# A decoder layer with Mamba, experts, cross-attention and FP8 FFN on one core: half of values × Wo moved into the scan, the sums of the experts moved into the attention pipeline

## The chip, the core and the metric

The kernel runs on one core of one Trainium2 chip, as one program. The metric is the time of one execution on the device in microseconds (us). A core has a matrix engine (TensorE, PE in the profile, with its weight loads as PEld), a vector engine (VectorE, DVE), a scalar engine (ScalarE, ACT), a general one (GpSimd, POOL) and SyncE (SP), which issues transfers. Each runs its own list of instructions in order, and they wait for each other on semaphores. Transfers (DMAs) are issued from an engine's list and then run beside all of them. SBUF is the on-chip memory, PSUM the memory that TensorE writes to.

## The reference

The input is `x` [4, 256, 256], four sequences of 256 tokens with 256 features, and a context of 4 × 64 positions with 128 features. Cut to what matters:

```python
# 1 Mamba mixer, then experts
xz = rmsnorm(x) @ in_proj.T                  # 256 -> 1024
xc = silu(causal_conv(x_half)); dt, B, C = split(xc @ x_proj.T)   # then rmsnorm of each
dt = softplus(dt @ dt_proj.T + dt_b)
h_t = h_{t-1} * exp(dt_t * A) + dt_t * x_t * B_t                  # DI = 512, N = 16
y = (sum_n h_t C_t + xc * D_param) * silu(z)
r = y @ out_proj.T + x; flat = rmsnorm(r)
moe = sum over the top 2 of 8 experts e:  p_e * ((silu(flat @ w1[e].T) * (flat @ w3[e].T)) @ w2[e].T)
x = layernorm(x + moe)
# 2 cross-attention, 16 heads of 128
q, k = rmsnorm(x @ Wq), rmsnorm(ctx @ Wk);  v = ctx @ Wv
x = layernorm(x + softmax(q k^T / sqrt(128)) v @ Wo)
# 3 gated FFN of 704, operands rounded to FP8 by row scales
x = layernorm(x + ffn(x))
```

## The kernel before

The 1024 tokens are 8 tiles of 128; `x_sb` holds all of them in SBUF. The stages follow each other, and the trace shows their bounds:

1. Prologue (0 to 60 us): norms, in_proj, convolution of the first half.
2. Scan (60 to 318 us): 64 steps `i`, the list `SL`; a step is one half of the tokens (`h`, 512 tokens), two of four chunks of channels (`c0`) and one state `n`. `M` = 32 is the first step of the second half. A step has `da` on ScalarE (L587), `dbx` on POOL (L595), the scan `hs` on VectorE (L654), its product with C, `hc`, on VectorE (L662) or, in 14 steps, POOL (L679), and the sum over states `py` on TensorE (L644). The row of B for a step, `bB`, comes by a DMA on SP three steps ahead (L577). Beside it runs `fill`, a chain of generators: work of the other stages cut into pieces by `yield`, of which each step takes one. All pieces share a pool of one PSUM bank, `ps1`, so a piece's matmuls can begin when the copy out of the piece before is done. In it are the second half's convolution and dt, then (from step M + 2) out_proj of the first half, its routing (`after_scan`), and in steps M + 18 to M + 21 the first two chunks of out_proj of the second half (`out_part`, matmuls p_op L426).
3. Rest of routing, keys and tables (318 to 402 us). K is folded with Wq here; the result, m_d, lies in HBM (a quarter, one sequence, is `mb`, 1 MB).
4. Expert slots (402 to 613 us): 23 slots of 128 token places, each with gate and up matmuls (p_gu L1121), transposes (p_hTa L1139, p_hTb L1144) and the down matmul (p_hTb L1151), and a write of the result `y` to `ys_d` in HBM (L1160).
5. Combine and values (613 to 650 us, L1207 to L1252). Each token's two expert rows are gathered from `ys_d` by 16 indirect DMAs on POOL (`yg`, L1214, two per tile). VectorE adds them with their gates (L1227), then a layernorm (L1233, L64 to L66, L1240). Beside it `prep_v` folds V with Wo for the attention: per group of `GQ` = 4 heads, `p_vT` = ctx · Wv (L814), a copy `vT` (L819), `p_vw` = v · Wo (L829), a copy to `vw_sb` (L835). Its weights (`cT_v`, four `wv_t`, four `wo_t`), Wq (`wq_sb`, L1193) and two `mb` (L1195) are loaded on SP when the last slot begins; the FFN's weights (L1218 to L1222) follow on SP.
6. Attention and FFN (650 to 855 us, L1258 to L1407): a software pipeline over tiles, in whose step `i` stand `stage_scores(i)`, `stage_attend(i - 1)`, `stage_up(i - 2)` and `stage_down(i - 3)`. Scores has the transposes p_x1T (L1274) and their copy x1T (L1275), p_q (L1280) with squares and their sums (L1285, L1286), p_sc (L1295) times the norm, and v minus its maximum on POOL (L1306). Attend multiplies with `vw_sb` (p_av L1327).

In the scan, the slots and the combine stage PE, DVE, ACT and POOL run in the order in which the code is written (`manual_schedule`). SP's order, and that of everything in stage 6, is set by a scheduler. Pools with `side="right"` lie at the other end of SBUF and are closed and opened as a stack.

These lines order stage 5: all gathers first, nine pieces of values, then per tile the sum, the norm of the tile before and two more pieces, and the rest before stage 6.

```python
pv.send(psV)
for _ in range(9):
    next(pv)
for t in range(NT):
    combine(t)
    if t:
        normed(t - 1)
    next(pv, None)
    next(pv, None)
normed(NT - 1)
run(pv)
```

Of the kernel before, what the change touches and what calls it, by code (L numbers as in the profile page):

```python
# [10 lines left out]
F32 = mybir.dt.float32  # L11
# [38 lines left out]
def decoder_kernel(  # L50
# [128 lines left out]

    flat_d = dram.tile([T, D], F32, name="flat_d")  # L180
# [4 lines left out]
    zs = mb.tile([P, NC, T], F32, name="zs")  # L185
    xc = mb.tile([P, NC, T], F32, name="xc")
    dt = mb.tile([P, NC, T], F32, name="dt")
    dtx = mb.tile([P, NC, T], F32, name="dtx")
# [60 lines left out]
    def conv_part(h, xpad, ps, early):  # L249
        cs = slice(h * HALF, (h + 1) * HALF)  # L250
        cw, cb = col("conv_w"), col("conv_b")
        acc = a1.tile([P, 2, HB, L], F32, tag="conv", name="conv") if early else None
        for c in (2, 3, 0, 1):
# [7 lines left out]
            else:  # L261
# [9 lines left out]
                xc[:, c, cs], v, AF.Silu if early else AF.Identity, bias=cb[:, c : c + 1]  # L271
            )
        if not early:
            yield
            nc.scalar.activation(xc[:, :, cs], xc[:, :, cs], AF.Silu)
            yield

    def z_part(h, hsT, ps):
        for c in range(NC):
# [6 lines left out]
            nc.scalar.copy(zs[:, c, h * HALF : (h + 1) * HALF], pt)  # L286

    def dt_part(h, hsT, ps, early):
# [7 lines left out]
        for i2 in range(HT // 2):  # L296
            pt = ps.tile([P, HALF], F32, tag="ps", name="p_xp")
            for i in range(2):
                t = h * HT + 2 * i2 + i
                for n, c in enumerate((2, 3, 0, 1)):  # L300
                    nc.tensor.matmul(
                        pt[:, i * W : (i + 1) * W], xc[:, c, t * P : (t + 1) * P], xpT[:, c, :],
# [54 lines left out]
        w = dtx[:, :, cs]  # L357
        b = col("dt_b")
        pairs = [slice(0, 2), slice(2, NC)]
        if early:  # L360
# [5 lines left out]
            with tc.manual_schedule(engines={ET.DVE, ET.Activation}):  # L366
                for c, pt in enumerate(pts):
                    nc.scalar.activation(u[:, c, :], pt, AF.Abs, bias=b[:, c : c + 1])
                    nc.vector.tensor_scalar(dt[:, c, cs], pt, b[:, c : c + 1], 0.0, add, ALU.max)
                for c in pairs:  # L370
# [3 lines left out]
                    nc.vector.tensor_tensor(dt[:, c, cs], dt[:, c, cs], u[:, c, :], sub)  # L374
# [5 lines left out]
                nc.vector.tensor_tensor(dt[:, c, cs], dt[:, c, cs], w[:, c, :], add)  # L380
                nc.vector.tensor_tensor(dtx[:, c, cs], dt[:, c, cs], xc[:, c, cs], mult)

            return
        for c in range(NC):
# [4 lines left out]
            nc.scalar.activation(dt[:, c, cs], pt, AF.Relu, bias=b[:, c : c + 1])  # L389
# [12 lines left out]
        for c in range(2):  # L402
            nc.gpsimd.tensor_tensor(dt[:, c, cs], dt[:, c, cs], u[:, c, :], sub)
        yield
        next(zp, None)
        for c in range(2, NC):
            nc.gpsimd.tensor_tensor(dt[:, c, cs], dt[:, c, cs], u[:, c, :], sub)
# [3 lines left out]
    def last_of_dt(h, chunks):  # L411
        cs = slice(h * HALF, (h + 1) * HALF)
        for c in chunks:
            nc.gpsimd.tensor_tensor(dt[:, c, cs], dt[:, c, cs], dtx[:, c, cs], add)
            nc.gpsimd.tensor_tensor(dtx[:, c, cs], dt[:, c, cs], xc[:, c, cs], mult)
            yield

    def out_part(h, ps, ob, chunks):
# [3 lines left out]
        for i in range(HT):  # L422
            t = h * HT + i
            pt = ps.tile([P, HALF], F32, tag="ps", name="p_op")
            for c in chunks:
                nc.tensor.matmul(  # L426
                    pt[:, 0:D], zs[:, c, t * P : (t + 1) * P], opT[:, c, :],
# [154 lines left out]
    def decay(i):  # L582
        h, c0, n = SL[i]
        cs = slice(h * HALF, (h + 1) * HALF)
# [893 lines left out]
```

## Time and profile before

| what | us |
|---|---|
| median of 3 runs | 852.98 (850.94 to 855.36) |
| profiled execution | 856.38 |
| its span in the trace | 854.7 |
| prologue, to | 60 |
| scan, to | 318 |
| routing, keys, tables, to | 402 |
| expert slots, to | 613 |
| combine and values, to | 650 |
| attention and FFN, to | 854.7 |

A profile is one execution. "Busy" is the time in which an engine executes; what it waits for is inferred from semaphores. Instructions are named by their output tile and by the line of the kernel. A matmul of 32-bit numbers shows as two records, so counts of records are twice those of the code there. TensorE's clock is throttled in some stages; the granted clock is given as a share. Further numbers from the trace: `hs` takes 2.28 us and there are 64, `hc` 1.22 on VectorE and 2.35 on POOL, `dbx` 2.35, `da` 2 × 0.69. In the combine stage VectorE's pieces per tile are two sums of 0.48, 0.43, 0.18, 0.15, 0.16 and 0.40, and ScalarE has a square root of 0.20 and one table load of 1.28. The first tile's p_q starts at 650.09, the second's at 663.12, the third's at 679.59; later steps of the pipeline take some 22 us each, with VectorE busy 19.

### The profile page before, as it was taken

The page shows a single profiled execution, that of the slowest core. Times are in us where ns is not written, and L with a number is a line of the kernel's source. Part 1 is how long each engine was busy: PE and PEld are TensorE (multiplying, and loading weights), DVE is VectorE, ACT ScalarE, POOL GpSimd, SP SyncE. Part 2 cuts the span into 40 slices and gives each one's busy share as a digit, 9 for nine tenths or more (in the row PEclk, how much of TensorE's full clock was granted, in tenths as well). Part 3 has the DMA queues.
Part 4 walks back from the last instruction along what each step waited for, and adds up shares of the span by engine and source line. Part 5 has one row for each costly group of instructions (what it writes and reads, how often), then busy time and mean ns, then how long its engine had stood idle before and what let it go on. Part 6 is the DMA issues. An engine that isn't in the chain of part 4 may idle for free.

```text
span 854.7 us, 8109 instructions
## 1 busy us (share of the span) xinstructions
PE 685.7 (80%) x2449; PEld 383.5 (45%) x2449; DVE 569.1 (67%) x959; ACT 341.4 (40%) x564; POOL 385.9 (45%) x278
## 2 busy tenths in 40 slices
PE   3968868778656776747999999999986998999963
PEld 1533433324322323635555656556642554555541
DVE  4468799997899993663335454555144578888885
ACT  3386654755533323322221112112233555555533
POOL 7039878899766860022012332222060334444451
PEclk9999998999877997767999999999997999999985
DMA  4023322256521308943022544232690101000000
GB/s 153 1 74 86 99 65 69 83 156 205 168 87 44 104 25 298 397 142 104 25 72 17 67 55 66 39 54 56 204 393 16 49 1 49 7 6 7 8 6 19
DMA packets 54954, 76.43 MB, mean 89 GB/s; under 512 B 15872, under 2 KB 35072, under 8 KB 54144
## 3 DMA queue, kind: packets, MB, share of 16 engines
q1 hardware_dynamic: 48048, 64.11, 23.8%
q0 software_dynamic: 2320, 6.56, 5.2%
q10 hardware_dynamic: 4544, 5.24, 1.8%
q8 instruction: 21, 0.34, 0.2%
q14 instruction: 21, 0.17, 0.1%
HBM read 64.22 MB, written 11.67 MB: 89 GB/s over the span
## 4 chain that ended last, share of the span: by engine, by line
PE 45%; DVE 26%; POOL 12%; issue 7%; ACT 6%; DMA 3%; ACTq 0%; POOLq 0%; DVEq 0%
PE p_gu L1121 12%; PE p_hTb L1151 8%; DVE hs L654 6%; PE py L644 5%; POOL dbx L595 4%; PE p_q L1280 3%; PE p_m L774 2%; DVE hc L662 2%; PE p_cv L264 2%; POOL v L1306 1%; PE p_gu L1361 1%; DMA wk_t<-in_wk_dram 1%; POOL yg L1214 1%; PE p_sc L1295 1%; DVE ssq L1286 1%
## 5 line engine op out<-in xcount | busy, mean ns | idle before, releaser
L595 POOL TENSOR_TENSOR dbx<-dtx,bB 128x1024 f32<-128x1024 f32 x64 | 149.4, 2354 | 23.7 <-DVE hs L654 12.5
L654 DVE TENSOR_TENSOR_SCAN hs<-da,dbx 128x1024 f32<-128x1024 f32 x64 | 145.5, 2281 | 17.0 <-POOL dbx L595 8.6
L644 PE MATMUL py<-hc,ident 128*128 128x512 f32 x256 | 134.1, 656 | 3.6 <-DVE yd L615 2.0
L1121 PE MATMUL p_gu<-w,xT 128*128 x276 | 119.2, 569 | 2.0 <-ACT xT L1111 2.0
L587 ACT ACTIVATE da<-dt,a_neg 128x510 f32<-128x510 f32 x128 | 87.7, 688 | 77.6 <-DVE hs L654 75.4
L644 PEld LDWEIGHTS py<-hc,ident 128*128 128x128 f32 x256 | 52.9, 208 | 113.8 <-issue 101.0
L606 PE MATMUL pC<-bc,sel 96*128 96x512 bf16 x50 | 20.5, 409 | 66.1 <-DVE hc L662 65.3
L1121 PEld LDWEIGHTS p_gu<-w,xT 128*128 128x128 f32 x276 | 49.9, 194 | 44.0 <-issue 34.6
L1151 PE MATMUL p_hTb<-w2r,hT 128*128 (+1 forms) x276 | 67.9, 387 | 0.7 <-ACT hT L1140 0.7
L662 DVE TENSOR_TENSOR hc<-hs,pC 128x1024 f32<-128x1024 f32 x50 | 61.1, 1221 | 4.8
L1280 PE MATMUL p_q<-wq_sb,x1T 128*128 128x512 f32 x128 | 58.8, 613 | 4.8 <-ACT x1T L1275 4.8
L1151 PEld LDWEIGHTS p_hTb<-w2r,hT 128*128 128x128 f32 (+1 forms) x276 | 50.4, 189 | 19.1 <-issue 7.6
L1132 DVE TENSOR_TENSOR h<-sg,p_gu 128x704 f32<-128x704 f32 x23 | 20.4, 888 | 42.1 <-ACT sg L1130 42.1
L1140 ACT COPY hT<-p_hTa 128x512 f32<-128x512 f32 x23 | 13.5, 586 | 83.1 <-PE p_hTa L1139 76.0
L917 POOL DMA_INDIRECT xs<-flat_d,tok_i x23 | 22.7, 986 | 43.0 <-PE p_xT L1109 28.4
L1280 PEld LDWEIGHTS p_q<-wq_sb,x1T 128*128 128x128 f32 x128 | 24.4, 195 | 34.6 <-issue 26.9
L85 POOL TENSOR_TENSOR wgu<-wgu,w_m 128x512 f32<-128x512 f32 (+1 forms) x6 | 7.6, 1267 | 71.3 <-DVE w_m L84 71.3
L1147 DVE COPY hT<-p_hTb 128x128 f32<-128x128 f32 (+1 forms) x46 | 11.0, 281 | 41.4 <-PE p_hTb L1144 41.4
L679 POOL TENSOR_TENSOR hc<-hs,cB 128x1024 f32<-128x1024 f32 x14 | 32.9, 2350 | 8.9 <-issue 5.3
L1306 POOL TENSOR_TENSOR v<-v,st 128x1024 f32<-128x1024 f32 x8 | 15.2, 1902 | 48.0 <-DVE st L1305 48.0
L1285 ACT ACTIVATE q<-p_q 128x512 f32<-128x512 f32 x32 | 18.9, 594 | 34.1 <-PE p_q L1280 26.5
L1214 POOL DMA_INDIRECT yg<-ys_d,yrow_i x16 | 15.4, 965 | 37.2 <-PE p_vT L814 32.6
(331 smaller groups left out, 1278.0 us busy)
## 6 DMA issues: line engine op xcount, KB each, us to landing
bB<-b_d SPq DMA_DIRECT2D x64, 256.0 KB, 3.2
w<-in_w1T_dram SPq DMA_DIRECT2D x2, 2816.0 KB, 21.5
w<-in_w3T_dram SPq DMA_DIRECT2D x2, 2816.0 KB, 25.3
w2r<-in_w2T_dram SPq DMA_DIRECT2D x8, 640.0 KB, 5.6
m_d<-mst SPq DMA_DIRECT2D x8, 512.0 KB, 2.9
mb<-m_d SPq DMA_DIRECT2D x4, 1024.0 KB, 8.2
cB<-b_d SPq DMA_DIRECT2D x14, 256.0 KB, 3.3
ys_d<-y SPq DMA_DIRECT2D x21, 128.0 KB, 1.7
```

The lines of the kernel that those rows point to most:

```text
L587: nc.scalar.activation(das[i % 2][:, j, :, 1:], dt[:, c, cs].rearrange("p (b l) -> p b l", l=L)[:, :, 1:], AF.Exp, scale=a_neg[:, c * N + ...
L595: nc.gpsimd.tensor_tensor(dbxs[i], dtx[:, c0 : c0 + 2, h * HALF : (h + 1) * HALF], bBs.pop(i).unsqueeze(1).to_broadcast(two), mult)
L644: nc.tensor.matmul(ys[i][j], ident, hc[:, j, :], start=(n == 0), stop=(n == N - 1))
L654: nc.vector.tensor_tensor_scan(hs, das[i % 2].rearrange("p c b l -> p (c b l)"), dbxs.pop(i).rearrange("p c t -> p (c t)"), 0.0, mult, add,)
L662: nc.vector.tensor_tensor(hcs[i], hv, pcs.pop(i).unsqueeze(1).to_broadcast(two), mult)
L679: nc.gpsimd.tensor_tensor(hcs[i], hv, cBs.pop(i).unsqueeze(1).to_broadcast(two), mult)
L917: nc.gpsimd.indirect_dma_start(out=xs[s], out_offset=None, in_=flat_d, in_offset=bass.IndirectOffsetOnAxis(ap=tok_i[:, s : s + 1], axis=0),)
L1121: nc.tensor.matmul(pt[:, c, 0:w], x[:, k, :], w13[k][:, bass.DynSlice(ex[s], 1), o : o + w].rearrange("p e i -> p (e i)"), start=(k == 0), ...
L1151: nc.tensor.matmul(po, hT[:w, i, :], w2r[:w, i, bass.DynSlice(ex[s], 1), :].rearrange("p e d -> p (e d)"), start=(i == 0), stop=(i == NI - 1),
L1214: nc.gpsimd.indirect_dma_start(out=y, out_offset=None, in_=ys_d, in_offset=bass.IndirectOffsetOnAxis(ap=yrow_i[:, j, t : t + 1], axis=0),)
L1280: nc.tensor.matmul(pq, x1T[:, k, :], wq_sb[:, k, q * HALF : (q + 1) * HALF], start=(k == 0), stop=(k == KD - 1),)
L1306: nc.gpsimd.tensor_tensor(v, v, st[:, 0].unsqueeze(2).to_broadcast(full), sub)
```

## The change

Values × Wo is split in two. The heads 0 to 7 (groups 0 and 1) are done in the scan's `fill` chain, one piece a step (some steps take two), after the first half's routing. What they give is copied by ScalarE to a small buffer and written to HBM (`vw_d`, 8 writes of 256 KB on SP, `park`). The heads 8 to 15 stay where they were, behind the last slot. Their pieces use the PSUM pool of the attention pipeline. The two chunks of out_proj of the second half come after the values in the chain, in the last four steps of the scan. The tiles xc, dt, dtx of the first half move to a pool of their own on the right side (`h0p`), which is closed at step M + 2, four steps later than the pool that was closed there before; so w2's loads begin three steps later.

After the slots POOL issues the gathers of tiles 0 and 1, then the load of `vw_d` into `vw_sb` (2 MB), gathers of tiles 2 and 3, the FFN's weights (3 MB in six DMAs, before on SP), gathers of 4 and 5, the second `mb` (1 MB, before on SP), gathers of 6 and 7. The sums and norms of tiles 0 and 1 come before the pipeline; that of tile `i` + 2 stands in the pipeline's step `i`, ahead of `stage_scores(i)`.

```diff
@@ pools @@
+    vw_d = dram.tile([B, P, H // 4, D], F32, name="vw_d")
...
-    xc = mb.tile([P, NC, T], F32, name="xc")
-    dt = mb.tile([P, NC, T], F32, name="dt")
-    dtx = mb.tile([P, NC, T], F32, name="dtx")
+    h0p = h0ctx.enter_context(tc.tile_pool(name="h0p", bufs=1, side="right"))
+    hp = (h0p, mb)
+    xc = [hp[h].tile([P, NC, HALF], F32, name=f"xc{h}") for h in range(2)]
+    dt = [hp[h].tile([P, NC, HALF], F32, name=f"dt{h}") for h in range(2)]
+    dtx = [hp[h].tile([P, NC, HALF], F32, name=f"dtx{h}") for h in range(2)]
...
@@ ahead of the scan loop @@
+    def prep_v(vp, groups, put):
+        cT = vp.tile([P, B * S], F32, name="cT_v")
+        nc.sync.dma_start(cT, ctxT)
+        ws = {}
+        for q in groups:
+            wt = vp.tile([P, HALF], F32, tag="wv_t", name="wv_t", bufs=len(groups))
+            nc.sync.dma_start(wt, wv[:, q * HALF : (q + 1) * HALF])
+            w2 = vp.tile([P, GQ, D], F32, tag="wo_t", name="wo_t", bufs=len(groups))
+            nc.sync.dma_start(w2, wo[q * HALF : (q + 1) * HALF, :].rearrange("(h p) d -> p h d", p=P))
+            ws[q] = wt, w2
+        ps = yield
+        yield
+        for q in groups:
+            wt, w2 = ws.pop(q)
+            vT = vp.tile([P, GQ, B * S], F32, tag="vT", name="vT")
+            for j in range(0, GQ, 2):
+                pt = ps.tile([P, HALF], F32, tag="ps", name="p_vT")
+                for o in range(2):
+                    nc.tensor.matmul(
+                        pt[:, o * B * S : (o + 1) * B * S], wt[:, (j + o) * HD : (j + o + 1) * HD], cT,
+                        start=True, stop=True,
+                    )
+                yield
+                nc.scalar.copy(vT[:, j : j + 2, :].rearrange("p h s -> p (h s)"), pt)
+            for j in range(GQ // 2):
+                for b2 in range(B // 2):
+                    pt = ps.tile([P, HALF], F32, tag="ps", name="p_vw")
+                    for b in range(2):
+                        for o in range(2):
+                            bb = 2 * b2 + b
+                            nc.tensor.matmul(
+                                pt[o * S : (o + 1) * S, b * D : (b + 1) * D],
+                                vT[:, 2 * j + o, bb * S : (bb + 1) * S], w2[:, 2 * j + o, :],
+                                start=True, stop=True,
+                            )
+                    yield
+                    put(2 * b2, q * (GQ // 2) + j, pt.rearrange("p (b d) -> p b d", d=D))
+
+    def park(b, pr, v):
+        st = vp.tile([P, 2, D], F32, tag="vw_st", name="vw_st", bufs=2)
+        nc.scalar.copy(st, v)
+        nc.sync.dma_start(vw_d[b : b + 2, :, pr, :].rearrange("b p d -> p b d"), st)
...
@@ in the scan loop @@
+            if i == M + 2:
                 pctx.close()
+                h0ctx.close()
...
+                early_values = prep_v(vp, range(2), park)
+                next(early_values)
...
             if i == M + 2:
-                fill = itertools.chain(fill, out_part(0, ps1, ob, range(NC)), after_scan(0, ps1, ob, False))
-            if i == M + N + 2:
-                fill = itertools.chain(fill, out_part(1, ps1, ob, range(2)))
+                early_values.send(ps1)
+                fill = itertools.chain(
+                    fill, out_part(0, ps1, ob, range(NC)), after_scan(0, ps1, ob, False),
+                    early_values, out_part(1, ps1, ob, range(2)),
+                )
             next(fill, None)
-            if i > M and i % 3 == 0 and (i - M) // 3 < E:
-                load_w2((i - M) // 3)
+            if i in (M + 10, M + 15):
+                next(fill, None)
+            if i > M + 2 and i % 3 == 0 and (i - M - 3) // 3 < E:
+                load_w2((i - M - 3) // 3)
...
@@ in the last slot @@
-                pv = prep_v(vp, vw_sb)
-                next(pv)
+                late_values = prep_v(
+                    vp, range(2, H // GQ), lambda b, pr, v: nc.scalar.copy(vw_sb[:, b : b + 2, pr, :], v)
+                )
+                next(late_values)
                 nc.sync.dma_start(wq_sb, wq.rearrange("(k p) c -> p k c", p=P))
-                for b in range(2):
-                    nc.sync.dma_start(mbs[b], m_d[b].rearrange("p k h s -> p k (h s)"))
+                nc.sync.dma_start(mbs[0], m_d[0].rearrange("p k h s -> p k (h s)"))
...
@@ in place of the combine stage @@
+    def load_ffn():
         for j in range(2):
+            nc.gpsimd.dma_start(wgu[j], wgu_d[j])
+            nc.gpsimd.dma_start(wdn[j], wdn_d[j])
+        nc.gpsimd.dma_start(sgu_row, sgu_d.unsqueeze(0).to_broadcast([P, 2, I]))
+        nc.gpsimd.dma_start(sdn_row, sdn_d.unsqueeze(0).to_broadcast([P, D]))
...
+        def combine(t):
+            if t < NT:
+                for j in range(2):
+                    nc.vector.scalar_tensor_tensor(
+                        x_sb[:, t, :], ygs.pop((t, j)), g2[:, j, t : t + 1], x_sb[:, t, :], mult, add
+                    )
+                layernorm(x_sb, t, wk2)
+
+        with tc.manual_schedule(engines={ET.PE, ET.DVE, ET.Activation, ET.Pool}):
+            for t in range(NT):
+                for j in range(2):
+                    y = ygs[t, j] = wk2.tile([P, D], F32, tag="yg", name="yg", bufs=2 * NT)
+                    nc.gpsimd.indirect_dma_start(
+                        out=y, out_offset=None, in_=ys_d,
+                        in_offset=bass.IndirectOffsetOnAxis(ap=yrow_i[:, j, t : t + 1], axis=0),
+                    )
+
+                if t == 1:
+                    nc.gpsimd.dma_start(
+                        vw_sb[:, :, 0 : H // 4, :].rearrange("p b h d -> p b (h d)"),
+                        vw_d.rearrange("b p h d -> p b (h d)"),
+                    )
+                if t == 3:
+                    load_ffn()
+                if t == 5:
+                    nc.gpsimd.dma_start(mbs[1], m_d[1].rearrange("p k h s -> p k (h s)"))
+            late_values.send(ps)
+            for _ in range(8):
+                next(late_values)
+            combine(0)
+            for _ in range(3):
+                next(late_values)
+            combine(1)
+            run(late_values)
...
@@ in the pipeline loop @@
+                combine(i + 2)
                 vs[i] = stage_scores(i)
```

## The prediction

> **What bounds the kernel now.** I read the page's busy row first, then busy time by stage, then, for the stage that the change takes apart, its timeline, its chain of waits and its list of waits.
>
> ```profile
> PE 685.7 (80%) x2449; PEld 383.5 (45%) x2449; DVE 569.1 (67%) x959; ACT 341.4 (40%) x564; POOL 385.9 (45%) x278
> ```
>
> TensorE at 80% is an average. By stage (start:end, length, busy us of PE, PEld, DVE, ACT, POOL, granted clock, DMA share, GB/s):
>
> ```profile
> 253.00:305.00 52.00, 33.72 (x76) 15.35 (x76) 48.15 (x47) 17.94 (x26) 38.67 (x18) 0.82 0.24 72
> 402.00:613.00 211.00, 207.62 (x790) 123.27 (x790) 94.13 (x249) 41.80 (x81) 48.47 (x45) 0.99 0.33 55
> 613.00:650.00 37.00, 24.89 (x163) 15.53 (x162) 17.54 (x57) 15.72 (x34) 15.44 (x16) 0.87 0.80 305
> 650.00:680.00 30.00, 28.36 (x77) 14.38 (x78) 14.47 (x26) 13.16 (x21) 5.71 (x3) 0.94 0.10 36
> 733.00:821.50 88.50, 78.06 (x363) 47.88 (x362) 75.94 (x162) 49.41 (x79) 39.57 (x29) 1.00 0.02 7
> ```
>
> Rows: end of the scan (VectorE full, TensorE a third idle); expert slots (TensorE 98%); combine and values (no engine full, DMA 80%); start of the attention pipeline (TensorE full, VectorE half idle); its steady part (VectorE 86%, TensorE 88%). The 37 us of the third row are the ones to win.
>
> ```profile
> 613.61 0.33 ACTq L1160 DMA_DIRECT2D ys_d<-y  x1
> 622.23 0.95 POOL L1214 DMA_INDIRECT yg<-ys_d,yrow_i  x1 [32.64 <-PE p_vT L814]
> 629.03 0.48 DVE L1227 SCALAR_TENSOR_TENSOR x_sb<-yg,g,x_sb 128x256 f32<-128x256 f32 x1 [15.45 <-DMA yg<-ys_d,yrow_i]
> 648.90 0.69 PE L1274 MATMUL p_x1T<-ident,x_sb 128*128 128x128 f32 x2 [7.51 <-ACT vw_sb L835]
> ```
>
> Columns: start, duration, engine, line, tile, idle time before and its releaser. The last slot writes its result at 613.61; the first gather, G below, starts at 622.23. The releaser named there only came last: in the program the gather waits for that write, so the write took 8.6 us. Tile 0 of attention starts at 648.90. From the chain of waits:
>
> ```profile
> 634.73 0.94 POOL yg L1214
> 635.67 0.30 issue
> 635.98 5.87 DMA yg<-ys_d,yrow_i
> 641.94 0.50 DVE x_sb L1227
> ...
> 648.28 0.58 ACT vw_sb L835
> 648.90 0.70 PE p_x1T L1274 x2
> ```
>
> Sixteen gathers at 0.95 + 0.30 us stand in a row, then a landing of 5.87, then VectorE's sums of the last tiles, then the last values copy, and only then tile 0. Tile 0's two gathers land by 630; it waits for tile 7's. The waits of the stage (total, times, longest) say the same:
>
> ```profile
> DVE x_sb L1227 <- DMA yg<-ys_d,yrow_i: 16.7, 4, 15.4
> PE p_x1T L1274 <- ACT vw_sb L835: 7.5, 1, 7.5
> ```
>
> **What the Trainium skill says.** "DMA: Bandwidth & Descriptors", section "Anatomy of one DMA — SWDGE (gpsimd) path": a DMA issued by GpSimd costs about 2.0 us fixed plus bytes over 436 GB/s, and making its descriptors is a small, varying part. The trace has 2.8 us as the shortest landing of a gather, 5.9 as the median; and POOL's time for one hardly depends on its rows:
>
> ```profile
> 508.63 0.91 POOL L996 DMA_INDIRECT wgu<-in_w_gu_dram,idx_dn  x1 [0.30 <-issue]
> 509.84 0.95 POOL L917 DMA_INDIRECT xs<-flat_d,tok_i  x1 [0.30 <-PE p_wT L1024]
> ```
>
> The first moves 64 rows, the second 128. "Perfetto Trace Analysis", section "DMA Instruction — SWDGE (GPSIMD)", takes such an instruction's end as the end of its descriptors, not the arrival of data: agrees (0.94 against 5.87 above). "SBUF — State Buffer", box "DVE blocks DMA": GpSimd can't write descriptors while VectorE runs an operation in its two-port mode; no run yet shows plain loads from POOL beside a busy VectorE, so this is a risk, not a price. "ScalarE: Activation LUTs", section "What ACT_TABLE_LOAD costs": about 1.28 us; the trace has 1.28.
>
> **The change part by part.** Everything is against the profiled execution: 856.38 us, span 854.7; the median of the runs is 852.98, 3.4 less, and I carry the difference over unchanged.
>
> *G, the first gather.* In the changed order three matmuls of the late p_vT stand ahead of the last slot's second transposes, and wait for cT_v and wv_t. The first wv_t is issued at 606.47 and lands in 5.8 to 7.4 us (its tile's row: 5.8/6.6/7.4), so about 612.8, where TensorE would be there at 609: the slot's end moves by +3.3 + 0.7 (two more p_vT, at 0.24 a record and two records a matmul, with their weights). Queued behind are the slot's p_hTa/p_hTb, y and its write. Against that, the write then meets less: before, weights for attention and FFN were queued on SP up to 624.7; now SP carries 4.63 MB (cT, two wv, two wo, wq, mb0), which at 390 GB/s (the best two slices of the page have 393 and 397) are 11.9 us from 606, so nearly gone at 617.6. Landing 3 in place of 8.6: −5.6. Sum −1.6; I take −1.5 (−3.5 if wv_t lands early, +1 if the write gains only 3).
>
> *Tile 0's start.* Before G + 27.86 (first p_q at 650.09). After: the gathers of tiles 0 and 1 are the first four. Gather 2 issued at G + 2.5; landing 4 (2.8 to 5.9), two sums of 0.48, norm 1.32 with a table load of 1.28 that is exposed, square root 0.20, transposes 0.70, copy 0.38, small gaps about 0.8: G + 12.5 (11.6 to 14.5). The late values, half of 7.7 + 16.8 = 12.2 us (busy time of p_vT and p_vw in this stage), lie beside G's wait and landings on TensorE, which has nothing else. −15.4.
>
> *What is late next: POOL's queue.* It now holds 16 gathers, vw_sb (2 MB), six FFN loads (3 MB), mb1 (1 MB) = 24 DMAs, and behind them tile 0's v minus its maximum. With a DMA at b = 1.25 us it ends at G + 30; the maximum of tile 0 is done 14.9 after its first p_q (664.96 before), G + 27.4. Sums of tiles 4 to 7 stand on VectorE inside tile 1's squares (start about G + 25.5); the last gather lands G + 32 to 35. From first p_q to tile 2's took 29.5 us before (650.09 to 679.59), with VectorE busy 3.37 of 12.5 in the first step. I take +0.5 (−0.5 to +2.5). Each further us in b costs 8: from then on the queue is the bound. All of it in bytes, 8 MB with the gathers at 390 GB/s, takes 20.5 us, so bytes are not the limit.
>
> *Sums of tiles 2 to 7 in the pipeline.* The two sums of tiles 2 and 3 (0.96 each) fall in the first step's idle VectorE. The norms (0.43 + 0.18 + 0.15 + 0.16 + 0.40 = 1.32) of tiles 4 to 7 fall in steps 2 to 5, of 17 to 28 us, where VectorE is on the path (15.34 of 21.8 in 679–701, 27.85 of 32 in 701–733): 5.3, a quarter of it hidden: +4 (+1 to +5.3). The number of table loads stays.
>
> *Scan.* Added to steps 47 to 59: 4 p_vT pieces (3.84 us, 0.96 each), 8 p_vw pieces (8.4, 1.05 each), 12 ScalarE copies of 0.58, 8 writes of 256 KB and 1.6 MB of loads on SP. TensorE gets 12.2 in the first row's 18 idle us, less 4.1 of out_part's second half that leaves it; ScalarE gets 7.0 of 34 idle; DMA is at 24%. VectorE, the bound, gets nothing: hidden, though with 80% TensorE is no longer far from the step. Not hidden: out_part's second half, four matmuls of 1.03 each, now comes in the last four steps, where TensorE's tail (12 py, 314.11 to 319.42) sets the end: the last one's 1.03, and 1 for single waits: +2 (−2 since VectorE's wait of 2.57 us for p_op at 278.80 may go; +5 if all four p_op and a wait count). On SP each write stands ahead of later loads of bB, 0.33 us an issue; these are sent three steps ahead, and a landing takes 3.2.
>
> *Slots* keep their instructions but for the last one (counted under G).
>
> Sum: −1.5 − 15.4 + 0.5 + 4 + 2 = −10.4. Profiled execution 846.0; median 842.6, so **843**.
>
> **The rivals.**
> A, as summed: 843; own range 838 (G −3.5, norms +1) to 848 (queue +2.5, scan +5).
>
> B, POOL's queue becomes the bound. For it: plain loads of 2 MB have no row from POOL, and descriptors may starve; and the loads' order would put the gathers of tiles 2 to 7 behind 2, 5 and 6 MB. Against: 64 and 128 rows cost the same. With b = 2.3: 8 × 1.05 = +8.4, 851; b = 2.6 gives back everything (+10.8).
> C, slower: the pieces of values lie on the scan's step, because a single PSUM bank makes each wait for the copy before it and pulls py, and with it hc's buffers and VectorE, along. Price: 12.2 + 12 × 0.58 + 4 × 1.03 = 23.3, and 8 issues of 0.33 ahead of bB = 2.6; 25.9 in place of 2 gives 867. It decides once the scan grows by more than 16.7 (857.3). For it: a p_vw piece is as long as a p_op piece (1.03), and VectorE waited for one of those. Against: that wait came from the copy on VectorE, which here is on ScalarE; TensorE is a third idle, and the same bank carries a piece a step before the change with VectorE at 92%.
> D, more than forecast: norms hidden altogether (−4) or no delay of the last slot (−3.5): about 839 and below.
> That the change does not do what it says, all gathers still waited for by tile 0 through a shared buffer, is excluded: sixteen buffers, and sums in tile order.
>
> **How the numbers follow.** A 0.59, B 0.18, C 0.09, D 0.14. 0.5% is 4.3 us, about what can be told from no change: faster means below 848.7. A and D lie there, and 0.04 of B: 0.77. The rest of B: same, 0.14. C: slower, 0.09. The range 835 to 853 takes in A, most of D and the better part of B, leaving out C, b of 2.6 and above and a sum of D's two gains.
>
> **What would show it.** Tile 0's first p_q 12 to 13 us after the first gather and about 17 earlier than 650; VectorE's long wait for gathers split into one before tile 0 and little in tile 1; POOL's DMAs 1.25 apart, plain ones too; the scan's hs still back to back and its last py within 2 us of 319.4; pipeline steps 2 to 5 longer by about 1 each. Wrong would be: plain POOL loads of 2 us or more with v waiting behind them, hs with gaps in steps 47 to 63, or a first gather later than 624.

## The result, and the profile after

| | before | after |
|---|---|---|
| median | 853.48 (4 runs, 850.94 to 855.36) | 843.48 (4 runs, 842.79 to 845.77) |
| ratio, 95% interval | | 0.9868 [0.9843, 0.9894] |
| span of the profiled execution | 854.7 | 843.6 |

10.0 us less by the medians, 11.1 by the two traces, against a forecast of 10.4 (843). The granted clock is not the same in every execution of one kernel: the scan's last `yd` ended between 320.7 and 326.1 us in the traces of this study with the scan of before or of after (from 110 to 150 us the clock was 0.91 in before's trace and 0.84 in that of `late_only`, whose scan is the same). So single traces are compared below stage by stage, each stage from its own start. The page's busy row, and the same stages of the changed kernel's trace as were shown of before (start:end, length, busy us of PE, PEld, DVE, ACT, POOL, granted clock, DMA share, GB/s):

```profile
PE 683.3 (81%) x2449; PEld 379.0 (45%) x2449; DVE 563.2 (67%) x959; ACT 341.2 (40%) x564; POOL 391.2 (46%) x286
```

```profile
253.00:305.00 52.00, 44.13 (x143) 19.73 (x143) 46.15 (x37) 23.06 (x37) 44.10 (x21) 0.87 0.38 117
398.00:610.00 212.00, 209.00 (x798) 124.31 (x797) 94.41 (x250) 41.88 (x80) 47.69 (x44) 0.99 0.35 58
610.00:631.50 21.50, 12.04 (x76) 6.70 (x74) 4.69 (x15) 7.95 (x15) 10.20 (x12) 0.78 0.68 253
631.50:665.50 34.00, 29.87 (x76) 15.21 (x76) 21.46 (x43) 13.03 (x21) 15.89 (x16) 0.89 0.53 199
```

The combine stage is 21.5 us in place of 37; TensorE has 10.4 us more work in the scan's end, where it had been a third idle; the first two steps of the pipeline last some 34 us in place of 30, with VectorE busy for 21.5 in place of 14.5. Its timeline around the start of tile 0 (start, duration, engine, line, tile, idle time before and its releaser):

```profile
605.12 0.67 PE L657 MATMUL p_vT<-cT_v,wv_t 128*128 128x256 f32 x2 [0.41 <-DMA wv_t<-in_wv_dram]
...
610.43 0.33 ACTq L1167 DMA_DIRECT2D ys_d<-y  x1
...
619.17 0.95 POOL L1240 DMA_INDIRECT yg<-ys_d,yrow_i  x1 [32.56 <-DMA mb<-m_d]
...
622.21 0.48 DVE L1231 SCALAR_TENSOR_TENSOR x_sb<-yg,g,x_sb 128x256 f32<-128x256 f32 x1 [12.05 <-DMA yg<-ys_d,yrow_i]
...
623.88 0.83 POOL L1246 DMA_DIRECT2D vw_sb<-vw_d  x1
...
624.89 1.28 ACT L66 ACT_TABLE_LOAD   x1 [9.22 <-DVE ln_rs L65]
...
626.29 0.57 ACT L662 COPY vT<-p_vT 128x512 f32<-128x512 f32 x1
...
626.91 3.68 PE L669 MATMUL p_vw<-wo_t,vT 128*64 128x256 f32 x16 [9.18 <-ACT vT L662]
...
630.52 0.69 PE L1274 MATMUL p_x1T<-ident,x_sb 128*128 128x128 f32 x2
```

Read from above: the late p_vT waited 0.41 us; the write still took 8.7 us until the first gather. The releaser named there, mb's load, only landed last, 0.3 after the write; in `write_first` below the gather starts while that load is still under way. Tile 0 no longer waits for tile 7's gathers, but its last wait is again for the values, since a copy of vT stands on ScalarE behind the square root of tile 0's norm and TensorE idles 9.2 us for it. A plain load of 2 MB costs POOL 0.83 us, not more than a gather.

The stages of the profiled executions of all kernels in this study, from the timeline. "Keys" is from the end of the last `yd` to the first slot's p_xT; "to G" from the copy of the last `y` to the first gather; "to x1T" from there to tile 0's copy of x1T; "seven steps" from there to tile 7's:

| kernel | last yd | keys | to G | to x1T | seven steps |
|---|---|---|---|---|---|
| before | 320.7 | 78.0 | 9.1 | 27.4 | 140.5 |
| after | 321.1 | 73.1 | 9.4 | 12.1 | 148.0 |
| late_only | 325.8 | 75.5 | 5.9 | 27.6 | 140.1 |
| scan_only | 321.2 | 71.5 | 8.8 | 27.2 | 140.6 |
| write_first | 322.9 | 71.6 | 3.3 | 20.6 | 145.9 |
| values_first | 322.1 | 71.7 | 8.9 | 8.4 | 148.1 |
| no_norm | 323.9 | 71.2 | 9.4 | 12.0 | 143.5 |
| man3 | 321.6 | 71.2 | 9.0 | 8.4 | 148.8 |
| man3_wf | 326.1 | 74.8 | 3.3 | 12.4 | 146.6 |
| man4 | 325.8 | 71.8 | 9.0 | 8.7 | 145.3 |
| man4_wf | 321.7 | 71.5 | 3.3 | 12.3 | 144.6 |
| man4_wf_warm | 326.0 | 71.5 | 3.3 | 12.3 | 146.3 |
| warm_before | 322.4 | 74.8 | 9.1 | 27.5 | 140.5 |
| busy_scan | 329.9 | 78.1 | 8.6 | 27.8 | 140.7 |

So the 11.1 us of the traces are: scan +0.4, keys −4.9, slots +1.1 (214.4 to 215.6 from first p_xT to last `y`), to G +0.4, to x1T −15.4, steps +7.5, rest −0.2.

### The profile page after: what moved, and what is told of

It is laid out like the page before. It is cut to its first block, busy times and chain, and to the rows that moved or that the text cites. A ratio compares the mean times of both kernels' runs of the same rounds, so it can differ in the third digit from the quotient of the medians.

```text
span 843.6 us, 8099 instructions
## 1 busy us (share of the span) xinstructions
PE 683.3 (81%) x2449; PEld 379.0 (45%) x2449; DVE 563.2 (67%) x959; ACT 341.2 (40%) x564; POOL 391.2 (46%) x286
## 4 chain that ended last, share of the span: by engine, by line
PE 46%; DVE 25%; POOL 11%; ACT 6%; issue 5%; DMA 5%; SPq 0%; POOLq 0%; ACTq 0%; DVEq 0%
PE p_gu L1128 12%; PE p_hTb L1158 7%; PE py L692 5%; DVE hs L702 5%; POOL dbx L597 4%; PE p_q L1280 3%; DVE hc L710 2%; PE p_gu L1361 2%; PE p_m L831 2%; DMA mb<-m_d 2%; PE p_cv L269 2%; POOL v L1306 1%; DVE ssq L1286 1%; DMA wk_t<-in_wk_dram 1%; PE p_hTa L1146 1%
## 5 line engine op out<-in xcount | busy, mean ns | idle before, releaser
L692 PEld LDWEIGHTS py<-hc,ident 128*128 128x128 f32 x256 | 52.0, 205 | 99.8 <-issue 88.4
L1154 DVE COPY hT<-p_hTb 128x128 f32<-128x128 f32 (+1 forms) x46 | 11.1, 282 | 42.3 <-PE p_hTb L1151 42.3
L733 POOL TENSOR_TENSOR hc<-hs,cB 128x1024 f32<-128x1024 f32 x14 | 32.9, 2351 | 11.9 <-issue 8.0
L1361 PE MATMUL p_gu<-wgu,xqT 128*128 128x352 bf16 x128 | 25.8, 367 | 10.5 <-ACT xqT L1353 10.5
L1240 POOL DMA_INDIRECT yg<-ys_d,yrow_i x16 | 15.5, 969 | 38.3 <-DMA mb<-m_d 32.6
```

The costliest lines, as they stand in the source:

```text
L692: nc.tensor.matmul(ys[i][j], ident, hc[:, j, :], start=(n == 0), stop=(n == N - 1))
L733: nc.gpsimd.tensor_tensor(hcs[i], hv, cBs.pop(i).unsqueeze(1).to_broadcast(two), mult)
L1361: nc.tensor.matmul(pg[:, g, 0:HI], xqT[:, k, :], wgu[j][:, k, g, hs], start=(k == 0 and j == 0), stop=(k == KD - 1 and j == 1),)
```

## The experiments

Each ratio below is against executions of before that ran beside that kernel; their medians were 855.46 to 856.71, above the 853.48 of the table. So the kernels are compared by ratio and by trace, not by their times. The changed kernel itself was timed in the first set alone (0.9868). A trace is one execution of each.

**One half each.** `late_only`: the kernel before, with all four groups of values behind the slots and sums, gathers and loads as changed.

```diff
+                late_values = prep_v(
+                    vp, range(H // GQ), lambda b, pr, v: nc.scalar.copy(vw_sb[:, b : b + 2, pr, :], v)
+                )
...
+                combine(i + 2)
                 vs[i] = stage_scores(i)
```

> The kernel before with only the late part of the change: sums in the pipeline, FFN loads on POOL, all four groups of values behind the slots, no pieces in the scan. Theory (both halves are needed): all 24.4 us of values now stand on TensorE ahead of the first transposes of tile 0, so tile 0's p_q comes some 25 to 27 us after the first gather and not 12.5; about 3 us gained there are given back in the pipeline: 850 to 856. Rival (the row of gathers was all that mattered, the values are hidden anyway): p_q 12 to 15 us after the first gather, 843 to 846. The keys stage, from the scan's last yd to the first slot's p_xT, tells whether its 4.9 us of gain hang on the scan's pieces: as before (about 78) if so.

855.12, ratio 0.9978 [0.9956, 0.9999]: nearly nothing. Its chain of waits ahead of tile 0 (start, us, what):

```profile
633.72 3.68 PE p_vw L827 x16
...
645.33 3.60 PE p_vw L827 x32
648.93 0.37 PE p_x1T L1254 x2
```

From 633.72 on, TensorE's values stand ahead of tile 0 up to the last microsecond. But they start late. This is the first of them in the timeline, with the idle time before it:

```profile
633.72 3.68 PE L827 MATMUL p_vw<-wo_t,vT 128*64 128x256 f32 x16 [9.71 <-ACT vT L820]
```

TensorE idles 9.71 us for a copy of vT that stands on ScalarE behind the square root of tile 0's norm, as it idles 9.2 us in the changed kernel. So what is shown is that moving the sums brings no earlier start in this order of instructions. With all values ahead of the sums, as in `values_first` below, tile 0 might start up to 9.7 us sooner, some 18 after the first gather (an estimate from this wait); no run has tried that. Nothing was given back in the pipeline (140.1), against my expectation; the trace says why: while tile 0 waited, VectorE had done all the sums and half of the norms.

`scan_only`: the changed scan, and the combine stage of before with two groups.

```diff
-            for _ in range(8):
-                next(late_values)
-            combine(0)
...
+        for t in range(NT):
+            combine(t)
+            if t:
+                normed(t - 1)
...
-                combine(i + 2)
                 vs[i] = stage_scores(i)
```

> The scan of the changed kernel, and behind the slots the combine stage of before (all gathers and sums ahead of tile 0) with two groups of values. Theory (the gain is tile 0's start, the scan costs next to nothing): 852 to 854, or 848 to 850 if the faster keys stage (4.9 us) belongs to the scan's pieces; p_q of tile 0 still 27 to 28 us after the first gather. Rival (half of the values alone pays): p_q under 22 us after the first gather, 845 to 848. Rival (pieces lie on the scan's step): last yd later than 325.

850.37, ratio 0.9944 [0.9926, 0.9962]. Tile 0 starts 27.2 after the first gather: half of the values alone does not move it. Its timeline:

```profile
627.85 0.69 PE L1285 MATMUL p_x1T<-ident,x_sb 128*128 128x128 f32 x2 [9.84 <-ACT vw_sb L1199]
...
642.36 0.37 ACT L1286 COPY x1T<-p_x1T 128x256 f32<-128x256 f32 x1 [0.60 <-DVE x_sb L1251]
```

TensorE has transposed tile 0 by 628.5, but the copy x1T stands on ScalarE behind the square roots of all tiles' norms, the last at 641.55, and these wait for the row of gathers. And yet this half brings some 4.8 us by the times; of the 7.6 by which its trace is shorter, 6.5 are in the keys stage (71.5), whose instructions the change leaves alone. The two halves give 0.2% and 0.6% alone, 1.3% together, each in the order that it was run in.

**The write and tile 0's start.** `write_first`:

```diff
-                nc.sync.dma_start(wq_sb, wq.rearrange("(k p) c -> p k c", p=P))
-                nc.sync.dma_start(mbs[0], m_d[0].rearrange("p k h s -> p k (h s)"))
             run(down)
             next(fill, None)
+        nc.scalar.dma_start(wq_sb, wq.rearrange("(k p) c -> p k c", p=P))
+        nc.scalar.dma_start(mbs[0], m_d[0].rearrange("p k h s -> p k (h s)"))
```

> The changed kernel with the loads of Wq and of the first mb (3 MB) issued on ScalarE's queue behind the last slot's write of y. Theory (the write took 8.7 us because some 2.6 MB of loads stand in the DMA engines ahead of it): the write lands in 2.5 to 4, the first gather comes about 5 us earlier after y's copy, tile 0 about 4 earlier, since its gathers now meet those 3 MB; besides, the plan puts the exponential of tile 0 behind one square of tile 1 and not four, worth 4 in the second step: 834 to 838. Rival (a write on this queue takes 7.5 to 8.7 us whatever stands in front): the first gather stays 8.5 after the copy, 838 to 841.

846.06, ratio 0.9893 [0.9832, 0.9953]. The write was as the theory had it: issued at 609.14, first gather at 611.79. (`late_only` has the same by accident: its loads of Wq and mb were issued 0.3 behind the write, and the gather came 5.2 after it.) But tile 0 came 20.6 us after the gather, which neither theory had. From its chain of waits:

```profile
611.79 0.95 POOL yg L1240
...
616.50 0.82 POOL vw_sb L1246
617.32 0.30 issue
617.63 8.98 DMA yg<-ys_d,yrow_i
...
626.63 0.49 DVE x_sb L1231
...
628.47 0.42 DVE x_sb L76
...
629.03 0.41 PE p_x1T L1274 x2
```

The gather at 617.63 is tile 2's, behind the 2 MB load of vw_sb; the scheduler had put the sums of tiles 2 and 3 on VectorE ahead of tile 0's norm (L76), which thus waited for a landing of 8.98 us that is not its own. Another 3.0 us passed between the transposes and their copy x1T at 632.42, which stood on ScalarE behind the square roots of later norms and two copies of values. The expectation's side remark came out in part: with the exponential of tile 0 behind one square of tile 1, the second step took 18.09 in place of 21.01, but the third 18.48 in place of 16.80.

`values_first`:

```diff
-            for _ in range(8):
-                next(late_values)
+            run(late_values)
             combine(0)
-            for _ in range(3):
-                next(late_values)
             combine(1)
-            run(late_values)
```

> The changed kernel with all late values ahead of the sums of tiles 0 and 1 in the order of TensorE and ScalarE, so that the last copies of vT and vw do not wait behind the square root of tile 0's norm. Theory: TensorE's hole of 9.2 us is gone, p_x1T of tile 0 follows its norm, 3.5 us sooner after the first gather (9 in place of 12.5); 839.5 to 841.5 if the rest of the pipeline follows. Rival (the second step waits for the last gathers and POOL's queue, which do not move): the gain goes into that step, 842.5 to 844.

840.32, ratio 0.9834 [0.9768, 0.9899], and 8.4 us to x1T in place of 12.1 with the seven steps unchanged: the theory's number, and by the trace a gain that stays. The times alone do not tell it from the changed kernel (0.9868 [0.9843, 0.9894]). The line that was late, now:

```profile
624.95 0.69 PE L1270 MATMUL p_x1T<-ident,x_sb 128*128 128x128 f32 x2 [6.88 <-DVE x_sb L76]
```

Tile 0's transposes now wait for its own norm.

**The pipeline's 7.5 us.** The steps, from one x1T copy to the next:

| | 0 | 1 | 2 | 3 | 4 | 5 | 6 |
|---|---|---|---|---|---|---|---|
| before | 13.04 | 16.48 | 16.79 | 27.76 | 22.09 | 22.17 | 22.18 |
| after | 13.32 | 21.01 | 16.80 | 26.75 | 24.63 | 23.32 | 22.17 |
| no_norm | 11.26 | 21.20 | 16.80 | 27.77 | 22.09 | 22.19 | 22.17 |
| man3 | 13.66 | 16.13 | 21.29 | 27.59 | 24.63 | 23.32 | 22.16 |
| man4 | 13.34 | 16.08 | 21.07 | 25.28 | 23.81 | 23.53 | 22.17 |

`no_norm`:

```diff
-                layernorm(x_sb, t, wk2)
+                if t < 2:
+                    layernorm(x_sb, t, wk2)
```

> The changed kernel without the layernorm of the summed tiles 2 to 7 (so the output differs there): the six norms that the change put into the pipeline are left out. Theory (the norms of tiles 6 and 7 lie on VectorE's path in steps 4 and 5): these steps go from 24.6 and 23.3 us back to 22.1 and 22.2, steps 2 and 3 stay within 0.7 of 16.8 and 26.8, about 3.5 less in all. Rival (the norms are hidden and the longer steps come from the order of instructions): steps 4 and 5 stay above 23.

Steps 4 and 5 are 22.09 and 22.19, as the theory had it; step 0 is 2.1 shorter and step 3 is 1.0 longer, outside the 0.7 expected. Over all steps the norms cost 4.5 (148.0 to 143.5). It ran once, in 841.77.

Step 1 keeps its extra 4.5. The chain of waits of the changed kernel there:

```profile
645.00 7.15 PE p_q L1280 x16
652.17 0.60 ACT q L1285
652.78 1.28 ACT L1307
654.08 1.07 ACT v L1307
655.16 1.23 DVE st L1308
...
656.82 1.91 POOL v L1310
```

Tile 0's v was ready for its exponential at 648.98 (POOL's subtraction at 646.92, 2.06 long), but on ScalarE the exponential stands behind four squares of tile 1; before, it stood behind one. What this costs TensorE in step 1, and at the end the same p_av of before:

```profile
658.77 1.09 PE L1321 MATMUL p_aT<-ident,v 128*128 128x128 f32 x8 [3.21 <-POOL v L1310]
660.10 5.22 PE L1327 MATMUL p_av<-vw_sb,aT 128*128 128x256 f32 x16 [0.24 <-ACT aT L1324]
```

```profile
674.80 3.72 PE L1327 MATMUL p_av<-vw_sb,aT 128*128 128x256 f32 x16 [0.24 <-ACT aT L1324]
```

TensorE waits 3.2 for tile 0's v, and then p_av takes 1.5 longer, at a granted clock of 0.50 from 660 to 663 us (1.00 in before): together 4.7, about the extra of this step. `man3` takes values_first, writes the order of the first two tiles out by hand, and moves the FFN's loads to ScalarE:

```diff
+            g0, g1 = scores(0, vs), scores(1, vs)
+            next(g0)
+            combine(1)
+            load_ffn()
...
+            next(g1)
+            next(g1)
+            run(g0)
+            combine(3)
+            for t in range(4, NT):
+                if t > 4:
+                    next(g1)
+                combine(t, False)
```

> The changed kernel with the values first, and with the first two tiles' scores and all sums in an order written by hand: the exponential of tile 0 behind one square of tile 1, the sums of tiles 4 to 7 behind tile 0's softmax sum; the six FFN loads issued by ScalarE behind tile 0's transposes. Theory (the second step's extra 4.5 us come from the exponential's place behind four squares): the second step (from tile 1's x1T to tile 2's) goes from 21.0 to 16.5 to 17.5, tile 0 stays 8.4 after the first gather: 834 to 837. Rival (the second step waits for the last gathers or for POOL's queue): it stays above 19.5.

842.16, ratio 0.9836 [0.9791, 0.988], which is values_first's; the 834 to 837 of the theory was missed. Step 1 is 16.13, as the theory had it; step 2 is 21.29: of the 4.9 us, 4.5 came back one step later. I took that for a flaw of my order, tile 1's squares waiting behind the square root of tile 3's norm, and mended it in `man4`:

```diff
-            run(g0)
-            combine(3)
+            combine(3, False)
+            run(g0)
...
+            run(g1)
+            layernorm(x_sb, 3, wk2)
```

> As man3, but the squares of tile 1 no longer wait on ScalarE behind the square root of tile 3's norm (its sums stand ahead of tile 0's softmax sum, its norm behind tile 1's scores). Theory (man3 gave the second step's gain back in the third only because of that place): second step 16 to 17, third 16.8 to 17.5, all seven steps together 143 to 145 in place of 148. Rival (VectorE's added work is the bound, so what one step gains the next one loses): the seven steps stay at 147 to 149.

Step 2 is still 21.07, so this theory fell. The seven steps take 145.3, 2.7 less than after, between the two expectations. What one step gains the next one mostly loses: the place of the exponential says where the extra time shows, not that it is there. It ran once, in 842.32.

`man3_wf` and `man4_wf` are these two with the loads of write_first:

> The same, with Wq and the first mb loaded behind the last write of y. Theory (the write then lands in about 3 us, and no sum of a later tile stands ahead of tile 0's norm any more): first gather 3.3 after y's copy, tile 0's x1T 1 to 4 us earlier than in the run without this: 831 to 835. Rival (the gathers lose to Wq and mb what the write gains): tile 0 at the same time, 834 to 837.

> The same with Wq and the first mb behind the last write of y. Theory: first gather 3.3 after y's copy, tile 0's x1T 1 to 4 us earlier than without, seven steps 143 to 145: 831 to 835. Rival: steps at 147 or more, 835 to 838.

man3_wf: 836.61, ratio 0.9751 [0.9714, 0.9788], the best of the study and better than both kernels; the time is in the rival's range, 1.6 above the theory's. From the copy of `y` to x1T it takes 15.7 in place of man3's 17.4: the gathers start 5.7 earlier and lose 4 of that to Wq and mb. Its trace is of the slowest of its five executions (844.33, the others 835.56 to 836.70). man4_wf: 839.3, 0.9818 [0.9747, 0.9888], above both expectations; four runs from 834.7 to 843.9; its seven steps are 144.6, but the times do not tell it from man3_wf.

**The keys stage.** In `warm_before` TensorE gets extra matmuls where it waits there:

```diff
+                if q == 1 and m == 0:
+                    for _ in range(6):
+                        nc.tensor.matmul(pt[:, 0:D], ident, x_sb[:, 0, :], start=True, stop=True)
```

and 14 more of them ahead of p_tok.

> The kernel before with 20 extra matmuls whose results are overwritten (identity times tile 0 of x_sb), 6 where TensorE waits for the second wk_t in the keys stage and 14 where it waits for the slot table. Theory (the keys stage is longer before because TensorE's granted clock stays at 0.50 for 14 to 18 us after its wait of 4 us): the clock is near 1.0 from 338 to 354, the keys stage (last yd to first p_xT) falls from 76 to 78 to 71 to 74, 848 to 852 where before is 853 to 855. Rival (the scan's part shortens that stage by something other than the clock, such as its loads): the stage stays at 75.5 to 78, time within 1 us of before or longer by what the extra matmuls take.

853.07, ratio 0.9956 [0.993, 0.9983]; the stage took 74.8, between the two ranges. The clock was 0.90 or more until 346 us and 0.50 after, so the extra matmuls only put the fall off. `man4_wf_warm` has the same matmuls in man4_wf:

> The same again with the 20 extra matmuls in TensorE's waits of the keys stage. Theory (the clock after a wait is what the extra matmuls lift, with the scan's pieces too): 1 to 4 less than the run without. Rival (with the scan's pieces that stage is at its short length anyway, 71 to 73): within 1.

840.9, 0.9826 [0.9753, 0.9899], the stage 71.5 in both: the rival, nothing more to gain there. Last, `busy_scan`, before with TensorE's added load in the scan alone:

```diff
+            if M + 22 <= i <= M + 30:
+                pt = ps1.tile([P, HALF], F32, tag="ps", name="p_x")
+                for _ in range(5):
+                    nc.tensor.matmul(pt[:, 0:D], ident, x_sb[:, 0, :], start=True, stop=True)
```

> The kernel before with 45 extra matmuls in the scan (identity times tile 0 of x_sb into the fill chain's bank, 5 in each of steps M + 22 to M + 30, results not read): about the 12 us of TensorE work that the change puts there, but no loads, no writes and no copies. Theory (the scan's pieces shorten the keys stage by keeping TensorE busier before it): the keys stage falls to 71 to 73.5, the time 3 to 6 below that of before. Rival (TensorE's work in the scan has nothing to do with it): the keys stage stays at 75 to 78.5, the time within 1.5 of before or above.

865.92, ratio 1.012 [1.0086, 1.0155]. The keys stage stayed at 78.1, so by this one trace TensorE's added work in the scan is not what shortens it. The rest is a price for the forecast's rival C, since these pieces came out longer than meant. From its chain of waits:

```profile
289.15 1.72 PE py L644 x4
290.87 2.16 PE p_x L692 x10
293.03 1.72 PE py L644 x4
294.75 2.16 PE p_x L692 x10
...
297.12 1.72 PE py L644 x4
```

py, extra piece, py, extra piece: TensorE is the bound with nothing between, a step takes 3.9 to 4.1 us, and from the start of step 40 to the last `yd` it takes 109.0 in place of 99.7. The change's pieces take 0.86 to 1.05 there. In the changed kernel's chain of waits they are near that edge and at one place over it:

```profile
287.71 1.72 PE py L692 x4
289.43 0.86 PE p_vT L657 x4
290.29 1.72 PE py L692 x4
292.01 1.01 PE p_vw L669 x8
...
297.01 3.69 DMA vw_d<-vw_st
300.78 0.58 ACT vw_st L679
301.36 0.60 ACT da L589
301.99 0.70 ACT da L589
302.78 2.30 DVE hs L702
```

Pieces follow py without a gap, and the write issued at 297.01 lands after 3.69 us; the copy that needs its buffer waits, and ScalarE idles 2.69 of it with `da`, and so `hs`, behind the copy. "Hidden" was too strong, then: the scan pays, and gains elsewhere. Counted from the start of step 40, which leaves out what the clock did earlier, the last `yd` comes after 99.7 to 100.3 us in the three traces without pieces and 99.8 to 101.9 in the ten with them, 0.4 more by the medians. Within that, from step 40 to 44 the ten take 16.8 to 17.7 us (the three 15.3 to 15.5), and from there to step 63 75.5 to 76.7 (77.4 to 77.8).

## Why the prediction was right, and where its terms were off

The time (843.48 for 843), the direction and the main mechanism were right: tile 0 no longer waits for sixteen gathers. Neither half alone brings that in the order in which it was run; whether the late half could with its values first is open. But the sum came out so well partly because errors cancelled.

- *Tile 0's start, −15.4.* Measured −15.4 (27.4 to 12.1 for x1T). The size was right, its parts were not: the second gather was issued 1.26 after the first and not 2.5, its landing was 2.7 and not 4, and 3.7 went to the values that were said to lie beside. values_first shows the difference: 8.4.
- *G, −1.5.* Measured +1.5, the last slot and the write together, in these two traces. Five traces with this slot's end and this write have 223.3 to 225.0 from first p_xT to first gather, three of before's order 223.1 to 223.6, so by the medians it is nearer 0. Both halves of this term were mis-sized. The late p_vT waited 0.41 and the slots grew by 1.1 at most, not 4, since wv_t landed 3.2 after its issue. The 5.8 to 7.4 that I took came from the second and third of before's four loads of wv_t; the first one's landing is not in that trace. And the write gained nothing: I had it issued when the 4.63 MB would be nearly through, 11.6 us after the first of them, but as the slot was hardly held up it came 9.0 after (601.4 to 610.4), with about half of them still to land. write_first shows that this queue was the cause. (Two slips are small beside this: by the forecast's own times the wait for wv_t is 3.8 and not 3.3; and the page's KB have 1024 bytes, so the loads are 4.85 million bytes and 12.4 us, not 11.9.)
- *POOL's queue, +0.5, and norms, +4.* Measured +7.5 together. The norms cost 4.5 (no_norm), inside +1 to +5.3, though not in the steps that I named: my sign "pipeline steps 2 to 5 longer by about 1 each" failed, for step 2 stayed, step 3 fell by 1.0, and steps 4 and 5 grew by 2.5 and 1.2, while by no_norm 2.1 were paid in step 0. The rest, 3.0, is above the +2.5 given as the upper end. Without the norms step 0 is 1.8 shorter than before and step 1 is 4.7 longer, where TensorE waits for tile 0's v. The twelve sums, the waits for late gathers and the order on ScalarE all stand in that step; which of them is the price is not separated, since man3 and man4 only moved it. Rival B fell: plain loads took POOL 0.54 to 0.83 each, the last gather was issued at G + 26, and v minus its maximum began right behind the maximum. POOL did stop twice for an earlier load's landing, 1.0 and 1.5 us. In values_first, with tile 0 earlier, v does stand behind that row for 2.8 us (maximum done at 641.32, v begun at 644.16), though the exponential waits for the squares for longer still.
- *Scan, +2.* Measured +0.4, in the two traces and by the medians of all. Rival C fell for pieces of 1 us; busy_scan shows it come true at 2.16 us.
- *The keys stage* had no term at all, and gave −4.9 in the traces and some −4.8 by scan_only's times. This is the step that was missing: I had looked only at stages whose instructions change. Its TensorE work is the same, but at another clock. Two slices of 4 us of before, and the same of after (columns as above):

```profile
342.00:346.00 4.00, 4.00 (x21) 4.00 (x21) 2.04 (x6) 1.01 (x3) 1.30 (x2) 0.50 1.03 398
346.00:350.00 4.00, 3.06 (x13) 2.60 (x12) 1.50 (x2) 2.48 (x4) 0.73 (x1) 0.50 1.04 398
```

```profile
342.00:346.00 4.00, 3.60 (x31) 3.36 (x30) 2.81 (x9) 1.96 (x5) 1.10 (x2) 0.96 1.03 399
346.00:350.00 4.00, 3.24 (x15) 2.91 (x16) 2.21 (x7) 2.43 (x5) 0.94 (x1) 1.00 1.03 393
```

The clock is 0.50 in one and about 1 in the other at much the same busy share. What is shown: with the scan's half the stage took 71.2 to 73.1 in nine of ten traces (74.8 in the tenth), without it 75.5 to 78.1 in three; extra matmuls in its waits gave 74.8 and a kernel faster by 0.4%; extra matmuls in the scan left it at 78.1. Nor is it the length of the wait ahead of the slow stretch: TensorE waited 3.63 there for wk_t in before and 4.51 in the changed kernel. What it is in the changed scan that brings the clock back sooner stays open.

So in these two traces the terms G and pipeline were 3.0 each too favourable, and scan (1.6) and keys stage (4.9) made up for it. That the sum came within a microsecond is luck.

## What to carry to other kernels

A row of work ahead of a pipeline is best ended by giving the first tile only what it needs; check then, engine by engine, that nothing for later tiles stands ahead of it in any of the in-order queues, since here a copy of values, a sum and a gather each did, and in both single halves a copy on ScalarE behind a square root held tile 0 or its values. What is moved out of a wait into a running pipeline has to be paid there: twelve sums of 0.48 and six norms of 1.32 are 13.7 us of VectorE's time that had stood beside a wait, and the steps grew by 7.5. A write that others wait for should be issued before the big loads, not behind them, once nothing else holds up what waits for it: alone it gave no faster kernel (write_first), with the order of the first tiles written by hand it did (man3_wf against man3).

## What the runs showed of the hardware

A write of 128 KB took 8.7 us to the first gather behind loads of which some 2.5 MB had not landed (the 1.5 us slices of the DMA view from 610.5 have 416, 423, 431, 401 and 70 GB/s, 2.6 MB with the write), and 2.65 with none in front of it, though the loads were on another issuing queue. "DMA: Bandwidth & Descriptors" in the Trainium skill, section "Queues, rings and completion order", has the queues share the same engines and a semaphore rise only after every earlier write of such an engine; this agrees, though no run separates the two.

"TensorE: Matmul & The Clock Gate" of the same skill, section "Part 1: The HAM clock gate", says that the clock halves after an idle window of about 3.4 us, returns after a busy one, and that the window runs freely. The halving agrees (0.50 after a wait of 3.6 us in before). The return does not: TensorE was fully busy from 338 to 346 us in before, and the clock was 1.00 again only from 354. Part of that time were matmuls of 8 columns (3.4 us), and no run shows what counts as busy for the clock. Together with the scan's 5 us this makes single executions of one kernel differ by several us: 39 of before ran from 850.07 to 861.29, and man3_wf's traced execution, 7.7 above its median, has a scan 4.5 longer and a keys stage 3.6 longer than man3's trace. So a change of 1% needs its stages compared, or many runs.

A sum on VectorE that met POOL's work on v took up to 2.00 us in place of 0.48 (in the traces of after, no_norm, man3 and man4). It is not what the pipeline lost: in values_first no sum met it, and the seven steps took 148.1 all the same.
